# Graph attention, 32 graphs on one core: a softmax in two passes with finished weights, and a first gather that comes out as feature by target

## The chip, the cores and the metric

One core of one Trainium2 chip. The metric is the device time in microseconds (us) of one execution. Every kernel below was run several times beside the kernel before on the same chip. A ratio is the mean time of one kernel's runs over the mean of the other's runs of the same rounds, so it is not quite the ratio of the medians quoted beside it. Each profile is one execution. A record is one instruction in a trace; an fp32 product leaves two here (4096 records of L307 in the trace of before, for 2048 products). A turn is a transpose on TensorE. PSUM is the memory into which these kernels let TensorE write its products, and a PSUM tile is a named buffer in it. The granted clock is the share of TensorE's full clock that the profile records as given.

## The reference

32 graphs of 512 nodes with 512 features go through one block: layer norm and relu, then two graph attention layers, then the residual.

```python
def gat_layer(x, mask, W, a_src, a_dst, bias, concat):
    xl = (x @ W).reshape(B, N, H, F)
    asrc = jnp.einsum('bnhf,hf->bnh', xl, a_src)
    adst = jnp.einsum('bnhf,hf->bnh', xl, a_dst)
    e = leaky_relu(asrc[:, :, None, :] + adst[:, None, :, :], 0.2)   # source, target
    e = jnp.where(mask[..., None], e, -1e9)
    attn = softmax(e, axis=1)                                        # over the sources
    out = jnp.einsum('bsdh,bshf->bdhf', attn, xl)
    ...
h = elu(gat_layer(h, mask, W1, ..., concat=True))    # 4 heads of 256 features
h = gat_layer(h, mask, W2, ..., concat=False)        # 1 head of 512 features
```

All products are fp32. Per graph there are two projections (x·W1, h·W2) and two gathers (weights times projected features, summed over the sources).

## The kernel before

The instruction order of TensorE is fixed by the kernel's text; the other engines' is set by a scheduler. In round i, TensorE runs the first projection of graph i+1, the second gather of graph i-1, the second projection of graph i and the first gather of graph i+1. The softmax weights `p` are made beside that, unnormalised: source on the partitions, target along the row. The maximum comes from one pass with target on the partitions:

```python
# soft(): per head
for d in range(NT):
    nc.vector.tensor_tensor_reduce(out=junk, in0=asr[:, h, :], in1=MASKT[b][:, d, :], ...
        op0=OP.add, op1=OP.max, accum_out=mx[:, h - h0, d : d + 1])
...                                     # rows of adst - top: a small turn, to DRAM and back
for t in range(0, NT, 2):
    for j in range(2):
        nc.scalar.activation(p[:, t + j, :], rr[h][:, 0, :], AF.Exp, bias=sc[...])
        nc.scalar.activation(e2[:, j, :], rr[h][:, 1, :], AF.Exp, bias=sa2[...])
    nc.vector.tensor_max(pp, pp, e2)
    nc.vector.tensor_tensor(pp, pp, MASK[b][:, t : t + 2, :], op=OP.min)
```

The first gather has the weights as the stationary operand and gives target by feature. A column of ones in `xl` gives the sum of the weights. The result is divided by it into `z`, and TensorE turns `z` for the second projection:

```python
ps = psum.tile([P, 2, 512], F32, tag="mm", ...)            # two target blocks
for j in range(2):
    for s in range(NT):
        nc.tensor.matmul(ps[:, j, : FH + 1], p[:, s, d * P : (d + 1) * P], xl[:, s, h, 2 : W + 1], ...)
nc.vector.reciprocal(inv, ps[:, :, FH : FH + 1])
nc.scalar.activation(z[:, dp, :], ps[:, 0, :FH], AF.Copy, scale=inv[:, 0, :])
nc.vector.tensor_scalar_mul(z[:, dp + 1, :], ps[:, 1, :FH], inv[:, 1, :])
...
# turn(): four transposes of z into a PSUM tile, then elu:
nc.scalar.activation(e, ps, AF.Exp, bias=bias)
nc.vector.tensor_scalar(e, e, 1.0, -1.0, op0=OP.min, op1=OP.add)
nc.vector.scalar_tensor_tensor(H1[b][:, g, :], ps, bias, e, op0=OP.add, op1=OP.max)
```

The turns of the mask stand in pairs inside the first gather, those of the norm between the groups of the first projection.

## Time and profile before

| | before |
|---|---|
| median of 3 runs | 3693.56 us (3690.33 to 3694.57) |
| TensorE busy, share of the span | 93% |
| mean granted clock of TensorE | 0.976 |
| one round (29 rounds averaged) | 112.1 us |
| prologue, to the start of the second round | 146.8 us |

A line of a timeline has the start in us, the duration in us of a run of equal instructions, engine, source line, what is written from what, the shape and, in brackets, how long the engine stood idle just before and what ended that. Consecutive matmuls overlap at their ends (in the prediction's first fence a run of 3.63 us from 1573.66 is followed by one that starts at 1577.13, 3.47 us later), so intervals are read from one start to the next. The rest of the reading is in the prediction.

### The profile page before, as it was taken

What the parts mean: (1) busy time and instruction counts of PE and PEld (TensorE: products, weight loads), DVE (VectorE), ACT (ScalarE), POOL (GpSimd) and SP (SyncE); (2) the same over time, 40 slices, a digit from 0 to 9 for tenths busy, and PEclk for the clock granted to TensorE, in tenths of its full rate; (3) what the DMA queues carried; (4) which work ended last, traced back from release to release, by engine and by line L of the source; (5) the groups of instructions that cost most, each with busy time, mean ns of one, the idle gap of its engine ahead of it and who ended that gap; (6) DMA issues with size and microseconds to landing.
All of it is one profiled execution on the core that took longest, in us unless ns stands there. A gap on an engine that the chain in (4) does not pass through costs nothing.

```text
span 3691.1 us, 42808 instructions
## 1 busy us (share of the span) xinstructions
PE 3432.2 (93%) x16544; PEld 2948.3 (80%) x16544; DVE 2228.1 (60%) x4710; ACT 1338.1 (36%) x2305; POOL 220.8 (6%) x166
## 2 busy tenths in 40 slices
PE   4889999999999999999999999999999999999998
PEld 3678888888888888888888888888888888888886
DVE  5566555675656665555765565766566655556653
ACT  1343333443323443324433334433234433244331
POOL 0000000000000000000000000000000000000000
PEclk7899999999999999999999999999999999999999
DMA  5111222122222122221212221222221222211111
GB/s 165 38 63 66 83 82 71 55 83 72 81 78 72 61 80 76 80 78 64 69 66 84 82 71 55 84 72 81 78 72 61 81 75 81 76 55 56 66 61 52
DMA packets 115804, 269.86 MB, mean 73 GB/s; under 512 B 14992, under 2 KB 19984, under 8 KB 111504
## 3 DMA queue, kind: packets, MB, share of 16 engines
q1 hardware_dynamic: 115600, 267.12, 22.4%
q8 instruction: 130, 2.13, 0.2%
q14 instruction: 74, 0.61, 0.1%
HBM read 232.53 MB, written 34.54 MB: 72 GB/s over the span
## 4 chain that ended last, share of the span: by engine, by line
PE 52%; DVE 23%; ACT 15%; DMA 7%; issue 3%; SPq 0%; ACTq 0%; POOL 0%; DVEq 0%
PE pxl L271 24%; PE po L307 12%; DVE jk L217 9%; PE po L366 9%; ACT e L246 7%; ACT p L243 6%; DVE p L250 4%; DMA orr<-drr 4%; DVE p L251 3%; PE pxm L337 3%; PE pz L287 2%; DMA drr<-rrr 2%; PE pht L155 1%; DVE xr L373 1%; DVE z L314 1%
## 5 line engine op out<-in xcount | busy, mean ns | idle before, releaser
L307 PE MATMUL po<-xl,p 128*128 128x257 f32 x4096 | 968.1, 393 | 11.6 <-DVE p L251 11.6
L271 PE MATMUL pxl<-w_sb,ht 128*128 128x258 f32 x4096 | 921.7, 382 | 7.4 <-DVE j L101 7.4
L337 PE MATMUL pxm<-w_sb,h 128*128 128x257 f32 x4096 | 911.6, 382 | 0.0
L307 PEld LDWEIGHTS po<-xl,p 128*128 128x128 f32 x4096 | 795.0, 198 | 129.5 <-ACT e L246 13.6
L337 PEld LDWEIGHTS pxm<-w_sb,h 128*128 128x128 f32 x4096 | 776.3, 191 | 117.6
L271 PEld LDWEIGHTS pxl<-w_sb,ht 128*128 128x128 f32 x4096 | 766.1, 190 | 113.6 <-DVE j L101 8.0
L243 ACT ACTIVATE p<-orr,sc 128x512 f32<-128x512 f32 x640 | 456.4, 713 | 363.1 <-DMA orr<-drr 363.1
L217 DVE CUSTOM_DVE_ANT_0 jk<-oas,mt 128x512 bf16<-128x512 f32 x640 | 538.1, 841 | 55.3 <-DMA oas<-das 45.0
L250 DVE TENSOR_TENSOR p<-p,e 128x1024 f32<-128x1024 f32 x320 | 391.0, 1222 | 170.1 <-ACT e L246 170.1
L366 PE MATMUL po<-xl,p 128*128 128x256 f32 (+1 forms) x2048 | 456.8, 381 | 6.4 <-DVE p L251 6.4
L246 ACT ACTIVATE e<-orr,sa 128x512 f32<-128x512 f32 x640 | 455.4, 712 | 0.1
L275 ACT ACTIVATE xl<-pxl 128x516 f32<-128x516 f32 x256 | 153.9, 601 | 801.9 <-PE pxl L271 801.9
L366 PEld LDWEIGHTS po<-xl,p 128*128 128x128 f32 x2048 | 387.2, 190 | 67.0 <-issue 7.1
L251 DVE TENSOR_TENSOR p<-p,m 128x1024 f32<-128x1024 f32 x320 | 392.6, 1227 | 6.6
L344 ACT ACTIVATE xl<-pxm 128x514 f32<-128x514 f32 x128 | 74.9, 585 | 658.5 <-PE pxm L337 658.5
L313 ACT ACTIVATE z<-po,inv 128x256 f32<-128x256 f32 x256 | 119.9, 470 | 462.0 <-DVE inv L312 461.9
L362 POOL TENSOR_TENSOR xr<-xr,b_sb 128x512 f32<-128x512 f32 x128 | 187.5, 1470 | 1313.8 <-DMA xr<-in_x_dram 1101.9
L287 PE MATMUL pz<-identf,z 128*128 128x128 f32 x1024 | 175.4, 280 | 66.4 <-ACT z L313 40.2
L141 DVE BATCH_NORM_STATS2 stats<-x 128x6 f32<-128x512 f32 x128 | 88.6, 693 | 224.5 <-DMA x<-in_x_dram 224.5
L287 PEld LDWEIGHTS pz<-identf,z 128*128 128x128 f32 x1024 | 130.4, 142 | 113.1 <-ACT z L313 47.1
L294 DVE SCALAR_TENSOR_TENSOR h<-pz,b_sb,e 128x512 f32<-128x512 f32 x256 | 191.0, 746 | 10.9 <-DVE e L293 0.9
L279 DVE COPY sc<-xl 128x32 f32<-128x32 f32 x32 | 6.0, 187 | 303.1 <-ACT xl L275 303.1
(49 smaller groups left out, 1383.5 us busy)
## 6 DMA issues: line engine op xcount, KB each, us to landing
orr<-drr SPq DMA_DIRECT2D x160, 512.0 KB, 3.7
x<-in_x_dram SPq DMA_DIRECT2D x128, 256.0 KB, 2.7
adj<-in_adj_dram SPq DMA_DIRECT2D x128, 256.0 KB, 2.9
xr<-in_x_dram SPq DMA_DIRECT2D x128, 256.0 KB, 2.6
oas<-das SPq DMA_DIRECT2D x32, 1024.0 KB, 4.5
out_dram<-xr SPq DMA_DIRECT2D x128, 256.0 KB, 2.3
oas<-das SPq DMA_DIRECT2D x32, 256.0 KB, 3.2
w_sb<-in_L_gnn_W_dram SPq DMA_DIRECT2D x4, 512.0 KB, 8.1
```

The lines of the kernel that those rows point to most:

```text
L217: nc.vector.tensor_tensor_reduce(out=junk, in0=asr[:, h, :], in1=MASKT[b][:, d, :], scale=1.0, scalar=-BIG, op0=OP.add, op1=OP.max, accum_ ...
L243: nc.scalar.activation(p[:, t + j, :], rr[h][:, 0, :], AF.Exp, bias=sc[:, 0, h, t + j : t + j + 1])
L246: nc.scalar.activation(e2[:, j, :], rr[h][:, 1, :], AF.Exp, bias=sa2[:, h, t + j : t + j + 1])
L250: nc.vector.tensor_max(pp, pp, e2)
L251: nc.vector.tensor_tensor(pp, pp, MASK[b][:, t : t + 2, :], op=OP.min)
L271: nc.tensor.matmul(ps[:, j, :W], ht[:, k, t * P : (t + 1) * P], w1_sb[:, k, hp + j, :], start=(k == 0), stop=(k == KT - 1),)
L287: nc.tensor.transpose(ps[:, d * P : (d + 1) * P], z[:, d, f * P : (f + 1) * P], identf)
L294: nc.vector.scalar_tensor_tensor(H1[b][:, g, :], ps, bias, e, op0=OP.add, op1=OP.max)
L307: nc.tensor.matmul(ps[:, j, : FH + 1], p[:, s, d * P : (d + 1) * P], xl[:, s, h, 2 : W + 1], start=(s == 0), stop=(s == NT - 1),)
L337: nc.tensor.matmul(ps[:, j, : W - 1], h1[:, k, t * P : (t + 1) * P], w2_sb[:, k, j * (W - 1) : (j + 1) * (W - 1)], start=(k == 0), stop=(k ...
L362: nc.gpsimd.tensor_tensor(xr, xr, b2_sb, op=OP.add)
L366: nc.tensor.matmul(ps[:, j, : hi - lo], p[:, s, d * P : (d + 1) * P], v[:, s, lo:hi], start=(s == 0), stop=(s == NT - 1),)
```

## The change

The intent: no division after the first gather and no turns of `z`. For that the weights have to be finished (divided by their sum) before the gather, so the softmax gets a first pass with target on the partitions, which gives the maximum and the sum, and a second pass which makes the finished weights with source on the partitions. The first gather then takes `xl` as the stationary operand and 512 targets as the moving one, and its result is feature by target, as the second projection wants it. The turns of the mask move singly into the first projection, those of the norm into the second gather and second projection. The core of the diff:

```diff
+            for d in range(NT):                                       # first pass
+                nc.scalar.activation(e, self.asr[i][:, j, :], AF.Prelu, bias=ad[:, d : d + 1], alpha=SLOPE)
+                nc.vector.tensor_tensor_reduce(out=e, in0=e, in1=MASKT[self.b][:, d, :], ..., accum_out=low[...])
+                nc.scalar.activation(e, e, AF.Exp, bias=low[...], scale=-1.0, accum_out=tot[...])
+            nc.scalar.activation(tot, tot, AF.Ln)
...
-                    nc.scalar.activation(p[:, t + j, :], rr[h][:, 0, :], AF.Exp, ...)
-                    nc.scalar.activation(e2[:, j, :], rr[h][:, 1, :], AF.Exp, ...)
-                nc.vector.tensor_max(pp, pp, e2)
+                    nc.vector.scalar_tensor_tensor(p[:, u, :], rr[:, 0, :], lo[...], rr[:, 1, :], op0=OP.add, op1=OP.max)
+                    nc.scalar.activation(p[:, u, :], p[:, u, :], AF.Exp, bias=lo[...])
...
 def gather1(b):
-            for dp in range(0, NT, 2):
-                ps = psum.tile([P, 2, 512], F32, tag="mm", name=f"po{b}_{h}_{dp}", bufs=3)
-                ... (target by feature, reciprocal, z)
+            ps = psum.tile([P, 2, 512], F32, tag="mm", name=f"po{b}_{h}", bufs=3)
+            for f in range(FPH):
+                for s in range(NT):
+                    nc.tensor.matmul(ps[:, f, :], xl[:, s, h, 2 + f * P : 2 + (f + 1) * P], p[:, s, :], ...)
+                nc.scalar.activation(e, ps[:, f, :], AF.Exp, bias=bias)
+                nc.vector.tensor_scalar(e, e, 1.0, -1.0, op0=OP.min, op1=OP.add)
+                nc.vector.scalar_tensor_tensor(H1[b][:, g, :], ps[:, f, :], bias, e, op0=OP.add, op1=OP.max)
...
 def gather2(b):
+            if d % 2 == 0:
+                ps = psum.tile([P, 2, 512], F32, tag="mm", name=f"po2{b}_{d}", bufs=3)
+                nc.tensor.matmul(ps[:, d % 2, :], p[:, s, d * P : (d + 1) * P], v[:, s, 1 : DO + 1], ...)
+            nc.vector.tensor_tensor(xr, ps[:, d % 2, :], xr, op=OP.add)
```

## The prediction

> **What bounds the kernel now.** I read the page first: its busy line, its groups, its chain.

> ```profile
> PE 3432.2 (93%) x16544; PEld 2948.3 (80%) x16544; DVE 2228.1 (60%) x4710; ACT 1338.1 (36%) x2305; POOL 220.8 (6%) x166
> ```

> TensorE is busy nearly all the time, the others are far from full. Then the timeline of TensorE over one image; a round runs from one start of the x·W1 product (L271) to the next. Here is the end of one round:

> ```profile
> 1573.66 3.63 PE L307 MATMUL po<-xl,p 128*128 128x257 f32 x16
> 1577.13 0.60 PE L287 MATMUL pz<-identf,z 128*128 128x128 f32 x4
> 1577.56 3.63 PE L307 MATMUL po<-xl,p 128*128 128x257 f32 x16
> ...
> 1590.52 0.38 PE L173 MATMUL pm<-identb,m 128*128 128x128 bf16 x4 [0.51 <-DVE mt L176]
> 1590.74 3.69 PE L307 MATMUL po<-xl,p 128*128 128x257 f32 x16
> 1594.26 0.60 PE L287 MATMUL pz<-identf,z 128*128 128x128 f32 x4
> 1594.70 0.39 PE L173 MATMUL pm<-identb,m 128*128 128x128 bf16 x4
> 1597.17 0.38 PE L173 MATMUL pm<-identb,m 128*128 128x128 bf16 x4 [2.08 <-DVE mt L176]
> ```

> The reader is to see start times. 16 records of 257 columns take 1577.13 - 1573.66 = 3.47 us, 0.217 each; four turns take 0.43, 0.11 each. The brackets are all the idle time: in the round 1486.16 to 1597.39 they add up to 5.7 us. Rounds start at 255.36 and 3505.60, 29 rounds apart, so a round is **112.1 us**. The work before the second round takes 146.8 us, the first full round 108.6, the end after 3615.9 takes 75.2. So TensorE's own stream is the bound, with some 6% of waits. The durations that I use for the other engines and the DMAs come from the groups and the list of DMA issues:

> ```profile
> L294 DVE SCALAR_TENSOR_TENSOR h<-pz,b_sb,e 128x512 f32<-128x512 f32 x256 | 191.0, 746 | 10.9 <-DVE e L293 0.9
> L217 DVE CUSTOM_DVE_ANT_0 jk<-oas,mt 128x512 bf16<-128x512 f32 x640 | 538.1, 841 | 55.3 <-DMA oas<-das 45.0
> L246 ACT ACTIVATE e<-orr,sa 128x512 f32<-128x512 f32 x640 | 455.4, 712 | 0.1
> ...
> orr<-drr SPq DMA_DIRECT2D x160, 512.0 KB, 3.7
> ```

> The number after the busy time is the mean in ns of one instruction; the last one of a DMA line is its us from issue to landing. The two steps ahead of L294, from the groups split by shape, take 0.68 (exp, L292) and 0.42 (L293).

> [...]
> - [...] Here every fp32 product leaves two records (4096 for 2048 products), each of 0.217 us for 257 columns[...].
> - [...] VectorE stands idle for 5.04 us before the L250 at 1551.46, until ScalarE's exp is done, and nothing from behind slips in.
> - [...] the L217 pass takes 0.69 us, and 1.6 to 1.8 beside the bias add of L362.
> - [...] the built program has one table load, so I count nothing for tables.

> **The change, part by part, per round.**
> 1. *Removed:* 32 turns of z, 32 x 0.11 = 3.5 us of TensorE, their waits (about 2.2 us in that round), the z scaling, reciprocals.
> 2. *Wider products.* From 0.110 us at 128 columns to 0.2177 at 258 a column costs 0.00083 us; 512 columns make 0.2177 + 254 x 0.00083 = 0.4285. First gather: 64 x 0.4285 = 27.4 instead of 27.8; second: 32 x 0.4285 = 13.7 instead of 13.9. Gain 0.6.
> 3. *Moved:* mask turns stand singly between groups of the first projection, so their waits (2.6 us) go. Norm turns cost the same elsewhere.
> 4. *Added:* ScalarE's 512-wide passes go from 40 to 60 a round (one starts 0.61 us after another, so 37 us; with its other work some 55), VectorE trades the maximum of 1024 for four additions; now 69.6 a round, then 69.6 - 10 x 1.22 (maxima) - 5.8 (z and reciprocals) + 20 x 0.75 (additions) + some 4 of small steps, so about 70. Neither becomes the bound by its sum. There are eight small turn-and-DMA trips instead of five.

> Sum of TensorE's work: 27.9 + 13.7 + 27.8 + 27.4 + 1.8 (norm) + 1.2 (masks) + 0.9 (small turns) = **100.7 us**. By this alone a round would gain 11 us.

> 5. *New waits, and here I decide.* The first gather now keeps two feature halves in one PSUM tile, and the first half is read (exp, then two VectorE steps) before the second half is written. In the list of waits of the built program the second half starts with a wait for VectorE; in a copy that I built with a tile for each half it waits for ScalarE instead, which merely frees an old buffer. So TensorE waits for the reader of its own first half. Per head: 0.17 from the record's last column to its end, exp 0.68, e 0.42, h 0.75 and four hand-overs of 0.05: 2.2 us. The second gather pairs two targets in the same way and waits for the final addition (0.74): about 1.1, twice. Floor: 100.7 + 4 x 2.2 + 2 x 1.1 = **111.7 us**, no better than now.

> 6. *The queues make it worse.* I walked by hand through the program order of each engine with these durations, t = 0 at the start of a round. A trip of a small turn (0.35), its copy (0.3), the write (1.2 to 2.0 from its issue to the next one's in the DMA queue's timeline, I use 1.5) and the read (3.7) takes 6 us.
>    - Small turn of the first pair of heads after five groups of the projection, at 18.8; its rows at 24.7. Their first passes hold ScalarE, 8 passes a head and copies between, to about 38.
>    - The projection ends at 29.2. The first target block of the second gather is done at 32.6; its addition stands behind the third first pass of head 1, so from 34.6 to 35.3: TensorE waits 2.8. The second pair's copy comes after it, and its read stands behind an xr load that waits for the output to land: rows at 41.8. The addition of the third block stands behind the first pass that waits for these rows: 1.6 more. Together 4.4.
>    - First passes of heads 2 and 3 to 52; the rows of head 0 are there at 50, its finished weights at 57. Behind them the copy of head 1's turn: rows 62.7, weights 68.6; the copy for head 2 is taken within, at 67.4, rows 73.3.
>    - The copy for head 3 stands behind a norm statistic that waits for its load: 72.9; rows at 78.3, four additions to 80.9, the first minimum to 82.1.
>    - Behind that minimum stands the copy of layer 2's columns, whose small turn TensorE meets after the first half-head, at 81.0. With h of that half behind it too, the second half starts at 85.7: 4.6 lost.
>    - On ScalarE the whole first pass of layer 2 (rows at 89.5) stands ahead of the next head's exp: that head loses 4.9. The last two lose 2.2 each.

>    Sum 100.7 + 4.4 + 4.6 + 4.9 + 4.4 = **119 us**. I take **118**, as chosen middle: head 3 can come a little sooner, and contention can bring it later.

> Ends: the prologue gains, because the norm of the second image no longer blocks the first product (idle 21.4 us before 50.75), and loses by the longer softmax, where nothing hides it: the first half-head can start near 90 instead of 104.7 and then needs 37 us (27.4, 2.2 four times): 127 for 146.8, an estimate good to 8 us. The end: 76 for 75.2, the two pair waits more and nothing else. Total 127 + 31 x 118 + 76 = **3861 us**.

> **Rivals.**
> - *Only the work counts*: waits of point 5 are met early or not there. For it: TensorE is the bound and loses 4 us of work and 5 of waits. Then 102 to 104 a round: about 3400. Against: the built list of waits.
> - *The floor*: the halves wait, but DMA trips and queues are quicker than my walk. 112 a round, total about 3670, the same. Against: L217's mean of 0.84 against 0.69, so contention costs some 3 us a round, which can fall on the long softmax chain.
> - *Slower still*: contention, an accumulator read after each summed exp, and loads in the DMA queue push head 3 to 86 or more: 122 a round, near 3980.
> - *ScalarE or VectorE becomes the bound*: 55 and 70 us of work in 118 speak against it.

> **Range and chances.** Rounds of 113.3 to 121.7 us give 3715 to 3975. Slower by over 2% needs over 3767, a round above 115: 0.75. The floor, and rounds up to 115, give most of the 0.18 for the same. Faster needs the waits of point 5 to be absent: 0.07.

> **What would show it.** Point 2: records of 512 columns at 0.43 us spacing in L301 and L360. Point 5: idle time of TensorE before L301 put down to the h step (L310), two to five us, four times a round, and before L360 to the addition (L364). Point 6: idle before the small turn of layer 2, put down to VectorE. TensorE's busy share below 90%, ScalarE near 50%. If L301 follows itself without gaps, the prediction is wrong in point 5; if gaps are 2.2 us throughout, in point 6; if the first image ends well off 127 us, in the prologue.

The forecast's sum is 127 + 31 x 118 + 76 = 3861 us. The one table load is in the trace of after (L70, 1.28 us), and "contention" is the longer time of L217 beside L362 (in the trace of before 1.63 us at 1530.50 and 1.80 at 1539.34, 0.69 without it). The cause of that is not shown; the 3 us a round are an estimate from the means, 20 x (0.84 - 0.69). The hand-overs of 0.05 us are an estimate too; the trace of after has 0.03 to 0.06 (L308 ends at 1738.55, L309 runs from 1738.58 to 1739.01, L310 from 1739.04 to 1739.79, and TensorE goes on at 1739.85).

## The result, and the profile after

The changed kernel is correct and takes **4054.64 us** (median of 4 runs, 4041.43 to 4061.14) against 3691.94 us before (median of 4 runs): ratio 1.0977, 95% interval 1.0948 to 1.1007. It is slower by 9.8%, and outside the range of the prediction (3715 to 3975 us).

From the page after, the busy line and the group of the first gather (busy us, mean ns of one record, idle time of TensorE before it):

```profile
PE 3482.1 (86%) x12544; PEld 2278.3 (56%) x12544; DVE 2075.8 (51%) x4739; ACT 1754.1 (43%) x3489; POOL 230.0 (6%) x166
L301 PE MATMUL po<-p,xl 128*128 128x512 f32 x2048 | 1109.5, 699 | 345.2 <-DVE h L310 345.2
```

There are 4000 matmuls fewer, and TensorE is busy for 50 us more. The first gather stands idle for 345.2 us before its products, all of it for the h step. Now the end of one round in the timeline of TensorE after:

```profile
1697.60 3.60 PE L301 MATMUL po<-p,xl 128*128 128x512 f32 x8
1704.03 0.27 PE L196 MATMUL pas<-identf,sc 128*4 128x128 f32 x1 [2.83 <-DVE sc L345]
1706.46 8.83 PE L301 MATMUL po<-p,xl 128*128 128x512 f32 x16 [2.16 <-DVE h L310]
1719.72 8.83 PE L301 MATMUL po<-p,xl 128*128 128x512 f32 x16 [4.43 <-DVE h L310]
1730.58 3.70 PE L301 MATMUL po<-p,xl 128*128 128x512 f32 x8 [2.03 <-DVE h L310]
...
1739.85 5.40 PE L301 MATMUL po<-p,xl 128*128 128x512 f32 x8 [2.02 <-DVE h L310]
1745.08 3.64 PE L282 MATMUL pxl<-w_sb,ht 128*128 128x258 f32 x16
```

Two things are to be seen. Before each second half of a head TensorE stands idle until the h step of the first half is done, 2.0 to 4.4 us. And some runs after such a gap are long: 8 records take 3.60 us in the first line and 5.40 in the last but one, 16 take 8.83 where twice the first would be about 7.0. The stretches of the same round with the granted clock (columns: window in us, its length, busy us of PE, PEld, DVE, ACT, POOL with instruction counts, clock, DMA share, GB/s):

```profile
1706.40:1710.00 3.60, 3.54 (x5) 1.48 (x6) 0.01 (x1) 0.00 (x0) 0.00 (x0) 0.53 0.21 73
1710.00:1715.20 5.20, 5.20 (x13) 2.07 (x11) 2.55 (x7) 3.30 (x6) 0.00 (x0) 1.00 0.00 0
```

Right after the gap the clock is 0.53 over 3.6 us, then 1.00 (1710.00 to 1715.20); the 16 records take 8.83 us where sep_late, below, has 7.03: some 1.8 us lost in this stretch. The clock record of this trace has 103 half-clock stretches, 66 of 3.4 us and 28 twice as long. The mean clock of the whole run is 0.936, against 0.976 before.

The rest of the round, in the timeline of TensorE, has two short gaps in the second gather:

```profile
1656.22 3.70 PE L360 MATMUL po<-xl,p 128*128 128x512 f32 x8 [1.25 <-DVE xr L364]
...
1664.58 3.71 PE L360 MATMUL po<-xl,p 128*128 128x512 f32 x8 [0.67 <-DVE xr L364]
```

Why the small turn of layer 2 waited (the 2.83 us at 1704.03) is in the timeline of VectorE, in its program order:

```profile
1699.93 2.74 DVE L261 SCALAR_TENSOR_TENSOR p<-orr,lo 128x512 f32<-128x512 f32 x4 [0.24 <-DMA orr<-drr]
1702.59 1.22 DVE L269 TENSOR_TENSOR p<-p,m 128x1024 f32<-128x1024 f32 x1
1703.72 0.16 DVE L345 COPY sc<-xl 128x4 f32<-128x4 f32 x1
...
1705.68 0.73 DVE L310 SCALAR_TENSOR_TENSOR h<-po,b_sb,e 128x512 f32<-128x512 f32 x1
```

The copy of layer 2's columns (L345) stands behind head 3's additions, which start when their rows have landed, and behind its first minimum; h of the first half stands behind all of it. Its exp (L308) stands behind head 3's exps on ScalarE too: it starts at 1703.66, though the half was done at about 1701.2. And the 4.43 us before 1719.72 come from ScalarE's order:

```profile
1712.48 2.55 ACT L232 ACTIVATE l<-oas,sc 128x512 f32<-128x512 f32 x4
1714.93 0.71 ACT L239 ACTIVATE l<-l,low 128x512 f32<-128x512 f32 x1
...
1717.75 0.67 ACT L308 ACTIVATE e<-po,b_sb 128x512 f32<-128x512 f32 x1
```

The whole first pass of layer 2 stands ahead of the exp (L308) for which TensorE waits.

Rounds, read from the starts of L282: the second round begins at 140.36 us, the third at 253.17; the 29 that follow take 124.29 us each; the last one with a first gather starts at 3857.53, the end begins at 3976.58 and takes 79.1.

### The profile page after: what moved, and what is told of

It is laid out like the page before. It is cut to its first block, busy times and chain, and to the rows that moved or that the text cites. A ratio compares the mean times of both kernels' runs of the same rounds, so it can differ in the third digit from the quotient of the medians.

```text
span 4055.7 us, 35993 instructions
## 1 busy us (share of the span) xinstructions
PE 3482.1 (86%) x12544; PEld 2278.3 (56%) x12544; DVE 2075.8 (51%) x4739; ACT 1754.1 (43%) x3489; POOL 230.0 (6%) x166
## 4 chain that ended last, share of the span: by engine, by line
PE 45%; DVE 25%; ACT 15%; DMA 12%; issue 2%; POOL 1%; SPq 0%; DVEq 0%; POOLq 0%; ACTq 0%
PE po L301 22%; PE pxl L282 16%; DVE p L261 7%; DVE p L269 6%; ACT l L239 6%; PE po L360 5%; ACT l L232 5%; DMA oas<-das 4%; DMA orr<-drr 4%; DVE l L235 3%; DVE h L310 2%; DMA x<-in_x_dram 2%; ACT e L308 2%; DVE xr L364 1%; DVE hn L151 1%
## 5 line engine op out<-in xcount | busy, mean ns | idle before, releaser
L301 PE MATMUL po<-p,xl 128*128 128x512 f32 x2048 | 1109.5, 699 | 345.2 <-DVE h L310 345.2
L301 PEld LDWEIGHTS po<-p,xl 128*128 128x128 f32 x2048 | 444.0, 224 | 964.5 <-issue 528.8
L282 PE MATMUL pxl<-w_sb,ht 128*128 128x258 f32 x4096 | 931.8, 384 | 2.4 <-DMA adj<-in_adj_dram 1.6
L282 PEld LDWEIGHTS pxl<-w_sb,ht 128*128 128x128 f32 x4096 | 767.0, 190 | 126.5 <-issue 14.8
L235 DVE CUSTOM_DVE_ANT_0 l<-l,mt 128x512 f32<-128x512 f32 x640 | 432.1, 703 | 383.3 <-ACT l L232 383.3
L265 ACT ACTIVATE p<-p,lo 128x512 f32<-128x512 f32 x640 | 426.3, 716 | 450.7 <-DVE p L261 450.7
L308 ACT ACTIVATE e<-po,b_sb 128x512 f32<-128x512 f32 x256 | 174.9, 683 | 891.0 <-PE po L301 891.0
L360 PE MATMUL po<-xl,p 128*128 128x512 f32 x1024 | 472.7, 604 | 83.3 <-DVE xr L364 71.5
L239 ACT ACTIVATE l<-l,low 128x512 f32<-128x512 f32 x640 | 454.2, 711 | 87.4 <-DVE low L235 86.8
L232 ACT ACTIVATE l<-oas,sc 128x512 f32<-128x512 f32 x640 | 426.6, 710 | 97.5 <-DMA oas<-das 97.5
L261 DVE SCALAR_TENSOR_TENSOR p<-orr,lo 128x512 f32<-128x512 f32 x640 | 442.0, 752 | 49.4 <-DMA orr<-drr 49.4
L309 DVE TENSOR_SCALAR e<-e 128x512 f32<-128x512 f32 x256 | 108.7, 425 | 644.6 <-ACT e L308 644.6
L360 PEld LDWEIGHTS po<-xl,p 128*128 128x128 f32 x1024 | 188.4, 191 | 314.7 <-issue 201.3
L310 DVE SCALAR_TENSOR_TENSOR h<-po,b_sb,e 128x512 f32<-128x512 f32 x256 | 191.3, 747 | 5.9
## 6 DMA issues: line engine op xcount, KB each, us to landing
orr<-drr SPq DMA_DIRECT2D x160, 512.0 KB
oas<-das SPq DMA_DIRECT2D x64, 512.0 KB
```

The costliest lines, as they stand in the source:

```text
L232: nc.scalar.activation(e, self.asr[i][:, j, :], AF.Prelu, bias=ad[:, d : d + 1], alpha=SLOPE)
L235: nc.vector.tensor_tensor_reduce(out=e, in0=e, in1=MASKT[self.b][:, d, :], scale=-1.0, scalar=BIG, op0=OP.add, op1=OP.min, accum_out=low[: ...
L239: nc.scalar.activation(e, e, AF.Exp, bias=low[:, d : d + 1], scale=-1.0, accum_out=tot[:, d : d + 1])
L261: nc.vector.scalar_tensor_tensor(p[:, u, :], rr[:, 0, :], lo[:, 0, j, u : u + 1], rr[:, 1, :], op0=OP.add, op1=OP.max,)
L265: nc.scalar.activation(p[:, u, :], p[:, u, :], AF.Exp, bias=lo[:, 1, j, u : u + 1])
L282: nc.tensor.matmul(ps[:, j, :W], ht[:, k, t * P : (t + 1) * P], w1_sb[:, k, hp + j, :], start=(k == 0), stop=(k == KT - 1),)
```

## The experiments

**Theory A**: TensorE waits for the reader of its own first half, because both halves lie in one PSUM tile, and these gaps also bring the granted clock down. **Theory B**: the longer softmax chain with its trips through DRAM holds the round. **Theory C**: products of 512 columns are granted a lower clock by themselves.

| run | what | median us | ratio to before | clock |
|---|---|---|---|---|
| changed kernel | | 4054.64 | 1.0977 | 0.936 |
| sep_first | own tile for each half, first gather | 3524.55 | 0.9553 | 0.984 |
| sep_second | own tile for each block, second gather | 3995.50 | 1.0827 | 0.930 |
| sep_both | both | 3456.98 | 0.9373 | 0.977 |
| fill | shared tiles, useless products in the wait | 3933.96 | 1.0671 | 0.975 |
| order_halves | shared tiles, other order of halves | 3528.62 | 0.9575 | 0.980 |
| short_gap | shared tiles, half copied to SBUF first | 3780.27 | 1.0241 | 0.961 |
| cols_early | shared tiles, layer 2's columns copied earlier | 4049.77 | 1.0984 | 0.940 |
| sep_cols | sep_both and cols_early | 3388.69 | 0.9188 | 0.989 |
| sep_late | sep_cols, small turns of layer 2 later | 3327.84 | 0.9002 | 0.991 |
| b_masks | kernel before, turns of the mask moved alone | 3681.87 | 0.9963 | 0.979 |

All ran in 3 rounds and were correct; the kernel before had medians of 3687 to 3698 us beside them. The 95% intervals of the ratios are within 0.003 on either side.

**sep_first: a PSUM tile for each half of the first gather.**

```diff
-            ps = psum.tile([P, 2, 512], F32, tag="mm", name=f"po{b}_{h}", bufs=3)
             for f in range(FPH):
+                ps = psum.tile([P, 2, 512], F32, tag="mm", name=f"po{b}_{h}_{f}", bufs=3)
```

> Edit: in the first gather each half of the features gets a PSUM tile of its own (of the same size and tag), nothing else. Theory A (TensorE waits for the reader of its own first half, and the gaps bring the granted clock down): the waits of the first gather for the h step vanish but for what the small turn of layer 2 causes, granted clock back to 0.97, round near 109 us, total 3560 to 3640. Theory B (the longer softmax chain with its DMA trips holds the round): the wait only moves to the small turns, total above 3850. Theory C (512-column products are granted a lower clock by themselves): the gaps go, the clock in the first gather stays near 0.85, total near 3720.

3524.55 us, clock 0.984, a round of 107.3 us: 530 us faster than the changed kernel by a move of one line. Theory A is met with somewhat more than expected, B and C fall as main causes: the chain is as long as it was, and the 512-column products now run at full rate but for some stretches (half clock costs 0.76 us a round, 6.15 in the changed kernel).

**sep_second: the same for the second gather.**

```diff
-            if d % 2 == 0:
-                ps = psum.tile([P, 2, 512], F32, tag="mm", name=f"po2{b}_{d}", bufs=3)
+            ps = psum.tile([P, 2, 512], F32, tag="mm", name=f"po2{b}_{d}", bufs=3)
```

> Edit: in the second gather each target block gets a PSUM tile of its own, nothing else. Theory A: the two waits for the final addition (1.3 and 0.7 us a round) go, the first gather keeps its waits: total 3990 to 4055, the same or just faster. Theory B: no change within 0.5%, as TensorE arrives earlier and waits longer at the small turn of layer 2. Theory C: no change of the clock.

3995.50 us: the pairing in the second gather costs about 59 us, 1.9 us a round, which is what its gaps (1.25 and 0.67 us) add up to. This is within what theory A expected.

**sep_both: both edits.**

> Both edits: a PSUM tile for each half in both gathers. Theory A: TensorE's work of 100.7 us a round is left, with some 4 us of waits at the small turn of layer 2: round 105 us, total 3450 to 3560, faster than the kernel before by 4 to 6%. Theory B: above 3800. Theory C: near 3680 with the clock low in both gathers.

3456.98 us, a round of 105.3 us. The expectation of theory A is met (6.3% faster than the kernel before, where 4 to 6 was expected). From the waits of TensorE in this run (us in total, times, longest):

```profile
PE pas L196 <- DVE sc L345: 92.2, 30, 5.0
PE prr L196 <- DVE r L246: 20.1, 4, 7.3
...
PE po L301 <- DVE h L310: 2.0, 1, 2.0
```

The waits for h are gone (2.0 us in all, 345.2 before). What is left is the small turn of layer 2, 3 us a round: the part of the truth in theory B.

**fill: more work in the gap.** Shared tiles stay. Ahead of each second half TensorE computes two products of constants that nobody reads.

```diff
             for f in range(FPH):
+                if f:
+                    idle = psum.tile([P, N], F32, tag="tp", name=f"idle{b}_{h}", bufs=2)
+                    for k in range(2):
+                        nc.tensor.matmul(idle, identf, w2_sb[:, k, :N], start=(k == 0), stop=(k == 1))
```

> Edit: the changed kernel with its shared tiles, but ahead of each second half of the first gather TensorE computes two 512-column products of constants into a spare PSUM tile that nobody reads (4 records, 1.7 us of the 2 us wait). Theory A on the clock (a gap of 2 us is what lowers the granted clock): more work, yet faster: the half-clock stretches after the gaps shrink from 3 to 5 a round to one or none, granted clock above 0.96, total 3830 to 3930. If the clock has nothing to do with the gaps (theory C[...]): total 4050 or more, clock 0.94 or less.

3933.96 us, 121 us faster with 512 records more, clock 0.975. The time is 4 us above the range that theory A expected, the clock as expected. TensorE's timeline at the end of a round:

```profile
1672.44 1.88 PE L303 MATMUL idle<-w_sb,identf 128*128 128x512 f32 x4
1674.63 3.70 PE L307 MATMUL po<-p,xl 128*128 128x512 f32 x8 [0.31 <-DVE h L316]
...
1681.71 1.88 PE L303 MATMUL idle<-w_sb,identf 128*128 128x512 f32 x4
1683.90 3.70 PE L307 MATMUL po<-p,xl 128*128 128x512 f32 x8 [0.31 <-DVE h L316]
```

The second halves start no earlier after the first ones than they did (5.62 us here, 1678.28 to 1683.90; 5.63 in the changed kernel, 1734.22 to 1739.85), as they still wait for h, but these 8 records run at full clock: 3.70 us. So with gaps of 0.31 us in place of 2.03 and 2.02 the slow runs are gone here, and the mean clock is 0.975 in place of 0.936: the lowered clock goes with the gap, and is a cost of its own.

**order_halves: shared tiles, heads in pairs.** First half of head 0, first half of head 1, then the two second halves.

```diff
-        for h in range(H):
-            for f in range(FPH):
+        for h, f in [(q + j, f) for q in (0, 2) for f in range(FPH) for j in range(2)]:
```

> Shared tiles kept, but the order of the halves is changed: first half of head 0, first half of head 1, second half of head 0, second half of head 1, and so on; the reader of a half then has 3.4 us beside other work. Theory A (the gap costs, not the sharing as such): nearly as good as own tiles for the first gather alone, 3520 to 3640, clock above 0.97. A rival, that writing into a tile whose other half is read is slow by itself: above 3850.

3528.62 us, as good as own tiles in the first gather (ratios 0.9575 and 0.9553). TensorE waits for h only 14.0 us in all. So sharing a tile as such costs no more here than the 0.2% between these two; it costs where TensorE has nothing else to do while the first half is read (345.2 us of waits for h in the changed kernel).

**short_gap: a shorter reader.** ScalarE copies each half to SBUF, and exp and h read the copy.

```diff
+                z = work.tile([P, N], F32, tag="z", name=f"z{b}_{g}", bufs=2)
+                nc.scalar.activation(z, ps[:, f, :], AF.Copy)
-                nc.scalar.activation(e, ps[:, f, :], AF.Exp, bias=bias)
+                nc.scalar.activation(e, z, AF.Exp, bias=bias)
```

> Shared tiles and order kept; ScalarE first copies a half to SBUF, and exp and h read the copy, so that TensorE waits for one copy (about 0.9 us) instead of the 2 us to the end of h. Theory A, with the clock following the length of the gap (gaps of 1.3 and 0.7 us in the second gather left the clock at 1.00): hardly any half-clock stretch is left, clock above 0.965, total 3640 to 3780. If every gap of whatever length lowers the clock: clock below 0.95 and total above 3800.

3780.27 us and a clock of 0.961, just outside of what the first reading expected (above 0.965, up to 3780 us), and clear of the second (below 0.95, above 3800 us). TensorE's timeline shows why:

```profile
1606.70 10.04 PE L301 MATMUL po<-p,xl 128*128 128x512 f32 x16 [3.21 <-ACT z L309]
1617.43 3.70 PE L301 MATMUL po<-p,xl 128*128 128x512 f32 x8 [0.69 <-ACT z L309]
...
1625.37 3.70 PE L301 MATMUL po<-p,xl 128*128 128x512 f32 x8 [0.69 <-ACT z L309]
```

After gaps of 0.69 us the 8 records take 3.70 us, as at full clock; after 3.21 us, where the first pass of layer 2 still stands ahead on ScalarE, 16 take 10.04, where 7.03 is the time at full clock (in the whole trace, 16 of 23 such gaps are followed by a slow run).

**The length of the gap, over whole traces.** A run of n records of 512 columns at full clock lasts n x 0.4285 us + 0.17 for the last one's end (3.60 us for 8, 7.03 for 16 and 17.33 for 40 in the trace of sep_late). I call a run slow if it takes over 1 us longer, and count the runs right after a gap of TensorE (only gaps that end with these records; the small turns have theirs apart):

| gap | gather, traces | runs | slow |
|---|---|---|---|
| below 1 us | first: fill, short_gap, sep_cols | 168 | 0 |
| below 1 us | second: changed, sep_first, order_halves, short_gap | 111 | 0 |
| 1.0 to 1.5 us | second: the same four | 122 | 0 |
| 2.0 to 2.3 us | first: changed kernel | 96 | 63 |
| 2.7 to 3.3 us | first: fill, short_gap | 52 | 28 |
| over 3.5 us | first: changed kernel, fill, short_gap | 42 | 41 |

Of the 96 gaps, 31 stand right behind the small turn of layer 2, before which TensorE mostly stood idle as well: all 31 are followed by a slow run. Of the other 65, 32 are. Gaps between 1.5 and 2 us hardly occur in these traces.

| full-clock windows with idle time of | windows, before | followed by one at half clock | windows, changed kernel | followed by one at half clock |
|---|---|---|---|---|
| below 1.6 us | 975 | 0 | 888 | 0 |
| 1.6 to 2.0 us | 32 | 16 | 38 | 0 |
| 2.0 us and more | 16 | 16 | 103 | 102 |

In these two traces, then, the idle time that falls into one window sorts the cases better than the length of one gap. Of the 96 gaps of 2.0 to 2.3 us in the changed kernel, 68 belong to a window with at least 1.95 us of idle time, and 63 of these are followed by a slow run; of the other 28, with less in each of their windows, none is. A half-clock window with over 1 us of idle time is followed by another in all 61 cases of the two traces, one with less than 0.5 us in none of 132.

Half of the time that TensorE is busy at half clock is what I count as the cost of the clock: 6.15 us a round in the changed kernel (29 rounds), 0.76 in sep_first, 2.06 in fill.

**cols_early: the copy of layer 2's columns ahead of head 3, shared tiles kept.**

```diff
-                11: lambda: s1.second(3),
...
+            if 0 <= i < B and not last:
+                late = Soft(i, 2, cols2(i), ...)
+                late.columns(0)
             if s1:
                 for n in sorted(plan):
                     plan.pop(n)()
+                s1.second(3)
             rest(nm)
-            if 0 <= i < B and not last:
-                late = Soft(i, 2, cols2(i), ...)
-                late.columns(0)
```

> Edit on the changed kernel with its shared tiles: the copy of layer 2's columns is put ahead of the last head's additions and minima, in the program order of VectorE. Theory A: the small turn of layer 2 no longer waits (2.8 us a round), but the second half waits for the h step all the same (about 2.1 us from the end of the first half), so 1 to 3 us a round are won: total 3950 to 4030, clock still 0.94. Theory B (the softmax chain holds the round): no change or a gain above 5%.

4049.77 us: the same. This missed the gain that I expected of 1 to 3 us a round; no change is what I had written for theory B. The timeline shows that a wait moved, and not that the softmax chain holds the round. The end of a round on TensorE:

```profile
1697.74 0.27 PE L196 MATMUL pas<-identf,sc 128*4 128x128 f32 x1 [0.71 <-DVE sc L345]
1702.06 8.83 PE L301 MATMUL po<-p,xl 128*128 128x512 f32 x16 [4.05 <-DVE h L310]
```

The turn waits 0.71 us instead of 2.83, and the second half 4.05 instead of 2.16, together 4.76 instead of 4.99. The h step of the first half stands behind the same additions and minima of head 3, so one wait took the place of the other.

**sep_cols: own tiles and the early copy.** Without the wait for h the same move counts.

> A tile for each half in both gathers, and the columns of layer 2 copied early. Theory A: the last steady wait of TensorE (3 us a round, with a half-clock stretch of some 3 us after it) goes, the round falls to the sum of TensorE's work, 101 to 102 us: total 3230 to 3320, clock near 0.985. Theory B: the wait moves to another place, total above 3400.

3388.69 us, clock 0.989, a round of 103.1: 68 us better than sep_both, though not the 3230 to 3320 that I expected. The waits at the small turn fell from 92.2 to 46.7 us, not to zero. The expected total was also too low for its own round: the next run has a round of 101.07 us and still takes 3328.

**sep_late: the small turns of layer 2 one half-head later.**

```diff
-                    if n == 0 and late:      # rows, first pass
+                    if n == 1 and late:
-                    if n == 5 and late:      # turn
+                    if n == 6 and late:
```

> Own tiles in both gathers and early columns, and the small turns of layer 2 one half-head later (after the second and the seventh half). Theory A: the last waits at that turn (47 us) and before the first gather (11 us) go, as VectorE has 3.4 us more: total 3310 to 3350. If the later turn makes the weights of layer 2 late for the second gather of the next round: 3390 or more.

3327.84 us, as theory A expected, ratio 0.9002 to the kernel before: the version that beats both. TensorE's first gather in this kernel:

```profile
1508.85 7.03 PE L301 MATMUL po<-p,xl 128*128 128x512 f32 x16
1515.71 0.27 PE L196 MATMUL pas<-identf,sc 128*4 128x128 f32 x1
1515.82 17.33 PE L301 MATMUL po<-p,xl 128*128 128x512 f32 x40
1532.99 0.27 PE L196 MATMUL prr<-identf,r 128*8 128x128 f32 x1
1533.10 3.60 PE L301 MATMUL po<-p,xl 128*128 128x512 f32 x8
1536.54 3.64 PE L282 MATMUL pxl<-w_sb,ht 128*128 128x258 f32 x16
```

No brackets. 16 records take 1515.71 - 1508.85 = 6.86 us, 0.429 each, and a round 101.07 us.

**b_masks: one part of the change alone, on the kernel before.** The turns of the mask stand singly in the next first projection; norm and softmax stay.

```diff
-            if d % 2:
-                yield
+            yield
...
                     step(nm)
+                    step(mt)
```

> The kernel before with one part of the change alone: the turns of the mask stand singly between the groups of the next image's first projection instead of in pairs inside the first gather. If the moved turns are worth the waits that the profile of before shows for them (75 us of idle before the mask turns): 3600 to 3630, 2% faster. If TensorE then waits elsewhere: above 3660. None of the clock theories bears on it, as those gaps are short.

3681.87 us, 0.4% faster: a fifth of what the waits promised. TensorE's waits in this run:

```profile
PE pm L173 <- ACT ht L156: 49.1, 60, 0.9
...
PE pm L173 <- DVE mt L176: 2.0, 1, 2.0
```

The mask turns no longer wait for their own evacuation, but for that of the norm turns, which share the two PSUM buffers and stand in the same place. The change moved both, and in it the wait for mt is 5.2 us in all. That the two moves belong together is likely, but no run moved both on the kernel before.

## Why the prediction was wrong

It named the direction and the cause; the size was off by 194 us.

1. *Turns of z removed*: right.
2. *Wider products, 0.4285 us a record*: right, 0.429 where TensorE runs without gaps.
3. *Mask turns*: right for the change as a whole (waits for mt 75.3 us before, 5.2 after), but b_masks shows that the mask turns moved alone win 0.4%.
4. *ScalarE and VectorE*: 1754.1 / 32 = 54.8 us a round, as predicted (55), and 2075.8 / 32 = 64.9 (70 predicted). ScalarE's share of the span is 43%, where near 50% was predicted. Each summed exp (L239) is followed by a read of the accumulator, recorded with 0.19 us; consecutive summed exps start 0.71 us apart (1715.64 to 1716.34 and 1717.05), plain ones 0.61 (in the trace of before, L243 at 1551.33 and L246 at 1551.94). L235, the successor of L217, takes 703 ns in the mean and not 841, 2.8 us a round of the 5.
5. *The wait for the reader of its own half*: right: 2.03 us of idle time and the 0.17 of the last record's end are the 2.2 predicted. sep_first and order_halves show the cause.
6. *The queues*: right in place. In the round shown above, counted from its start at 1622.18, head 3's additions start at 77.8 us (78.3 predicted) and the second half at 84.3 (85.7). The round has gaps of 1.25 + 0.67 in the second gather (4.4 predicted), 2.83 + 2.16 at the turn of layer 2 (4.6), 4.43 (4.9) and 2.03 + 2.02 (4.4): 15.4 us, or 16.6 with seven ends of 0.17 us, 18.3 predicted. The second gather was put at twice what it takes; taking 118 for the sum of 119 hid part of that.

**The step that failed** is the sum: "Sum of TensorE's work ... = 100.7 us" was taken as the same whatever gaps lie in it. With the gaps gone it is right (101.07 us in sep_late). With them, the granted clock is half for a while after many of them (63 of the 96 gaps of 2.0 to 2.3 us and all 32 longer ones before the first gather), and the same work takes 6.2 us a round more. The waits came out nearly as predicted: 118 - 100.7 = 17.3 us a round, the ends of the last records included. Measured, as totals of the changed kernel's trace over 32: 10.8 (waits for h) + 2.7 (turn of layer 2) + 2.2 (second gather) = 15.7 of idle time, and 1.2 for the ends of seven gaps, together 16.9. So 101.1 (work) + 16.9 (waits) + 6.2 (clock) = 124.2, measured 124.29. I had taken 118: 29 x 6.29 = 182 of the 194 us.

The rest: the prologue took 140.4 us instead of 127. Its first gather begins at 92.84, near the 90 predicted, but takes 47.5 us instead of 37: its first wait alone is 8.49 us, with a slow stretch behind it. With own tiles in the first gather it ends at 124.2. The first full round took 5 us less than predicted, the last two pieces 4 more.

The clock was in reach of the prediction: the trace of the kernel before already has 33 half-clock stretches at a mean clock of 0.976 (103 at 0.936 after), and the prediction makes no use of them.

## What to carry to other kernels

If a PSUM tile is filled half by half and each half is read as soon as it is done, look in the built program whether the second half waits for the reader of the first; give each half its own tile, or put other TensorE work between the halves (waits for h: 345.2 us with shared tiles, 2.0 with own tiles, 14.0 with the other order). In the changed kernel the repeated gaps of 2 us on TensorE cost more than 2 us, because records after them ran at half clock (63 of the 96 gaps of 2.0 to 2.3 us were followed by a slow run): count such gaps with a surcharge, and fill them if they can't be closed. Add up gaps that lie close together: in the traces of before and of the changed kernel 2.0 us of idle time within one window of 3.413 us was followed by half clock in 118 of 119 cases, less than 1.6 us in none of 1863. And when a wait is removed, look for the instruction next in the same engine's queue before counting the gain (cols_early took 2.83 us at the turn down to 0.71, and the wait behind it went from 2.16 to 4.05).
